# Scores moved directly behind a visit's transpositions, and first blocks' transposed tiles packed four to a PSUM bank, in a fused encoder and decoder layer

## The chip, the cores and the metric

The kernel runs on one NeuronCore of a Trainium2 chip. Its time is the device time of one execution in microseconds (us). Three executions of the kernel before gave 2728.57, 2730.44 and 2730.65, a median of 2730.44. Beside these stands one profiled execution, from which all rows of the profile come. Everything is computed in fp32.

## The reference

An encoder layer runs over a short context (2 x 77 x 512), and a decoder layer over 2 sequences of 2048 tokens, both with 16 heads of 32 and a feed-forward part of 2048. Cut to what matters:

```python
D, H, DFF, MD = (512, 16, 2048, 128)

def _rel_bias(emb, qlen, klen):
    rp = arange(klen)[None, :] - arange(qlen)[:, None]
    bucket = where(rp < 0, minimum(-rp, MD - 1), minimum(rp, MD - 1) + MD)
    return emb[bucket].transpose(2, 0, 1)

def _mha(xq, xkv, w_in, b_in, w_out, b_out, bias):
    q, k, v = ...                     # projections, 16 heads of 32
    scores = einsum('bhqd,bhkd->bhqk', q, k) / sqrt(32) + bias[None]
    attn = softmax(scores, axis=-1)
    out = einsum('bhqk,bhkd->bhqd', attn, v)
    return out.transpose(0, 2, 1, 3).reshape(Bq, Tq, D) @ w_out.T + b_out

x = src                               # the context, 2 x 77 x 512
x = x + _mha(_ln(x, ...), _ln(x, ...), ..., enc bias)
x = x + relu(_ln(x, ...) @ ff1.T + b1) @ ff2.T + b2
memory = x
y = tgt                               # 2 x 2048 x 512
yn = _ln(y, ...)
y = y + _mha(yn, yn, ..., _rel_bias(dec_rel_self, 2048, 2048) + causal)
y = y + _mha(_ln(y, ...), memory, ..., _rel_bias(dec_rel_cross, 2048, 77))
y = y + relu(_ln(y, ...) @ ff1.T + b1) @ ff2.T + b2
```

The change lies in the causal self-attention of the decoder. The relative bias is a constant for keys 127 or more positions back, so only the last two key tiles of a row of tiles need the bias added.

## The kernel before

**Units and pieces.** A sequence of 2048 tokens is cut into four blocks of 512 tokens, m = 0 to 3; the text calls them first to fourth block. The 16 heads make four groups g of four heads, and a block has four row tiles t of 128 tokens. One (sequence, m, g, t) is a unit, 128 of them (line 329). Unit (m, t) sees 4m + t + 1 key tiles of 128, and `pieces` (line 315) cuts these into pieces of at most four tiles. `stream` lists all pieces in order.

**The four operations on a piece.** `scores` (line 357) takes four banks of PSUM, one a head, and multiplies the queries of a head (32 rows of TensorE's array) with up to 512 keys into each (line 375). VectorE then reads each bank once, writes the scores to SBUF and reduces their maximum (line 384; line 391 for the last two tiles, with bias). After a unit's last piece one more reduction joins the maxima (line 401), and four exponentials on ScalarE, one a head, are put into a list, `late_exps`; `exps(k)` issues k of them (line 406). `turn` (line 412) transposes probabilities on TensorE, 128 x 128 at a time (line 426), into PSUM banks, and copies each bank to SBUF, on VectorE (line 431) or ScalarE (line 433). A bank normally holds one key tile of the four heads; in a first block it holds one head's key tiles, one to four. `values` (line 440) multiplies the transposed probabilities with the values (line 455) into a bank of its own, which is read out at the end of the visit.

**PSUM.** Eight banks make a ring (`bank`, line 180): each new bank is the one taken longest ago. TensorE waits where that bank has not been read yet.

**The order of the work.** It is written out by the main loop (from line 1883), one visit per pair of pieces of a unit. A unit of a first or second block has one visit; a unit of a third or fourth block has two (third block: seven or eight tiles, then 2, 2, 3 or 4; fourth: eight, then five to eight). Every engine runs its own instructions in this order. In a unit's last visit the order is: transpositions, then `slot(n + 1)`, then exponentials, then the scores of the unit two ahead (`score_next` for one piece, `score_two` for two), then the values. In an earlier visit there is no slot. `may_score` allows a piece only when the unit two before has turned the tiles whose place in SBUF it takes, since two units' probabilities alternate there.

**Slots.** `slot(n)` (line 1319) holds everything that is not attention between probabilities and values: first the light stages, then products, then late stages. Light and late stages are norms of later rows, the whole encoder (during the first sequence), the first part of the cross-attention, bias tiles, and sums and stores of weights for the feed-forward part; each has a planned slot. The products are the q, k, v and output projections of neighbouring blocks as one-level Strassen parts: `part_job` (products at line 1134) and `pair_job` (line 1048), with weights loaded two jobs ahead by `load_next` through SP's queue. `w2_store` and `w2_sums` (lines 1401 to 1432) prepare feed-forward weights on SP's queue and on POOL and reuse a buffer, so that the store of a half has to be issued ahead of the next sums.

After the last unit a stage of cross-attention and feed-forward follows, from about 1651 us of the span on, whose code is not touched.

Of the kernel before, what the change touches and what calls it, by code (L numbers as in the profile page):

```python
# [22 lines left out]
HC = P // HD  # L23
MB = 512
NMB = T // MB
TB = MB // P
# [28 lines left out]
def tile_encoder_decoder(ctx: ExitStack, tc: tile.TileContext, ins, out):  # L55
# [103 lines left out]
    with (  # L159
# [20 lines left out]
        def bank():  # L180

            ring.append(ring.pop(0))
            return psum[:, ring[-1], :]

        def in_turn(what, tile):
            i = count[what] % tile.shape[1]
            count[what] += 1
            return tile[:, i, :]
# [126 lines left out]
        def pieces(i):  # L315


            n = i + 1
            if n % 4 == 1 and n > 1:
                sizes = [4] * ((n - 5) // 4) + [3, 2]  # L320
            else:
                sizes = [4] * (n // 4) + ([n % 4] if n % 4 else [])
            out, k0 = [], 0
            for s in sizes:
                out.append((k0, s))
                k0 += s
            return out

        units = [(b, m, g, t) for b in range(B) for m in range(NMB) for g in range(NC) for t in range(TB)]
        stream = [(n, k0, kn) for n, u in enumerate(units) for k0, kn in pieces(u[1] * TB + u[3])]  # L330
# [78 lines left out]

        got = {}  # L410

        def turn(pieces):

            first = units[pieces[0][0]][1] == 0
            loads = []
            for n, k0, kn in pieces:
                ks = range(k0, k0 + kn)
                if first:
                    loads += [[(n, k, r) for k in ks] for r in range(HC)]
                else:  # L420
                    loads += [[(n, k, r) for r in range(HC)] for k in ks]
            for o, load in enumerate(loads):
                pt = bank()
                pts = in_turn("pts", pts_all).rearrange("p (x q) -> p x q", q=P)
                for x, (n, k, r) in enumerate(load):
                    nc.tensor.transpose(pt[:, ts(x, P)], state[n]["p"][r][:, k], ident)  # L426
                    got[n, k, r] = pts[:, x, :]
                w = len(load) * P
                free = pieces[0][0] == len(units) - 2 and (pieces[0][1] or o >= 4)
                if free or (o % 2 if first else o in (4, 6) if len(loads) == 8 else o >= (len(loads) + 1) // 2):  # L430
                    nc.vector.tensor_copy(pts[:, : len(load), :], pt[:, :w])  # L431
                else:
                    nc.scalar.copy(pts[:, : len(load), :], pt[:, :w])  # L433
                if not first and o == (7 if len(loads) == 8 else min(3, len(loads) - 1)):
                    exps(1)
            exps(HC if first else 0 if units[pieces[0][0]][1] == NMB - 1 else 1)

# [739 lines left out]
        NU = NC * TB  # L1177
        jobs = {n: [] for n in range(-1, len(units) + NU)}
        light = {n: [] for n in range(-1, len(units) + NU)}
        late = {n: [] for n in light}  # L1180

        for x, (b, m) in enumerate(blocks):
            u = x * NU
            first = m == 0
# [27 lines left out]
            for t in range(TB):  # L1212
                end = x == len(blocks) - 1
# [29 lines left out]
            for g in range(NC):  # L1243
# [4 lines left out]
                at = u + g * TB - 3  # L1248
# [67 lines left out]
            light[n].append(lambda kind=kind: wc_sums(sa_name[kind], True, spare, sa_from[kind]))  # L1316
            late[n + 1].append(lambda kind=kind: wc_store(sa_d[kind], spare))
        light[6].append(lambda: make_bias(2, rel, v))
        def slot(n):
            for f in light[n]:  # L1320
                f()
            for _, run, _ in jobs[n]:
                load_next()
                run(loaded[ran[0]])
                ran[0] += 1
            for f in late[n]:
                f()
            if n == 5:
                load_next()
# [62 lines left out]
        free = pp[:, 3 * HC * MB : END - 3 * HC * MB]  # L1392
# [28 lines left out]
        def w2_store(c, part):  # L1421

            def store(z0, z1, name, src):
                u = SUBS.index(name)
                nc.sync.dma_start(w2_d[z0:z1, u, :, ts(c, P)].rearrange("z p o -> p z o"), src)

            if part == 0:
                for n in ("11", "21", "22"):
                    store(0, 7, n, tens[:, :7, int(n[0]) - 1, ts(int(n[1]) - 1, P)])
            (z0, z1), t = list(ones.items())[part]  # L1430
            for k in range(4):
                store(z0, z1, f"T{k + 1}", t[:, k])
# [25 lines left out]
            late[u + 8].append(lambda dst=dst, z=z: wc_store(dst, z))  # L1458
        u = 2 * NU
        for c, k in enumerate((0, 2, 4, 10)):  # L1460
            light[u + k + 2].append(lambda c=c: w2_store(c, 1))
            late[u + k + 1].append(lambda c=c: w2_store(c, 0))
        for c, k in enumerate((0, 2, 4, 10)):
            light[u + k].append(lambda c=c: w2_sums(c))
        u = 6 * NU
# [381 lines left out]
        end = len(units)  # L1847
        size = [m * TB + t + 1 for b, m, g, t in units]
        turned_to, scored_to, at = {n: 0 for n in range(end)}, {}, [0]
# [11 lines left out]
        def score_next():  # L1861
            n, k0, kn = stream[at[0]]
            scores(n, k0, kn)
            scored_to[n] = k0 + kn
            at[0] += 1

        def score_two():

            n, k0, kn = stream[at[0]]
            at[0] += 1  # L1870
            both = may_score()
            at[0] -= 1
            if both and stream[at[0] + 1][0] == n and stream[at[0] + 1][2] < kn:
                scores(*stream[at[0] + 1])
                scores(n, k0, kn)
                scored_to[n] = size[n]
                at[0] += 2
            else:
                score_next()
                if both:  # L1880
                    score_next()
# [1 line left out]
        score_next()  # L1883
        score_next()
        slot(0)
        i = 0
        while i < len(stream):
            n = stream[i][0]
            pair = [p for p in stream[i : i + 2] if p[0] == n]
            while scored_to.get(n) != size[n]:  # L1890
                score_next()
            while any(u == n for u, _ in late_exps):
                exps(1)
            ends = pair[-1][1] + pair[-1][2] == size[n]
            turn(pair)
            if n == end - 2:
                for _, k0, _ in pair:
                    feed(k0 + 4)
            turned_to[n] = pair[-1][1] + pair[-1][2]
            third = units[n][1] == 2  # L1900
            if third and ends:
                exps(2)
            if ends and n + 1 < end:
                slot(n + 1)
            if not third:
                exps((0, 2, 1, 1)[units[n][1]])
            if may_score():
                if units[n][1] and (len(pair) > 1 or third):
                    score_two()
                else:  # L1910
                    score_next()
            if third and not ends:
                exps(1)
            values(pair)
            while may_score() and (len(pair) > 1 or units[n][1] == 0):
                score_next()
            if third and not ends:
                exps(1)
            i += len(pair)
# [68 lines left out]
```

## Time and profile before

| what | value |
|---|---|
| three executions | 2728.57, 2730.44, 2730.65 us |
| profiled execution | 2728.76 us, span 2726.9 us |
| granted TensorE clock, mean | 0.998 |
| instructions in the span | 68245 |
| TensorE matmuls / weight loads | 2707.0 us (99%) / 2214.9 us (81%), 26606 each |
| VectorE (DVE) | 1842.0 us (68%), 5402 |
| ScalarE (ACT) | 1534.6 us (56%), 2994 |
| GpSimd (POOL) | 1000.8 us (37%), 844 |
| HBM | 140 GB/s over the span |

All times inside the span are counted from its start. The first sequence's four blocks of self-attention begin at 28.4, 162.4, 370.1 and 590.0 us, the second's at 853.7, 991.2, 1185.2 and 1405.2; the last ends at 1651.1. The busy time of TensorE (PE) is modelled from when matmuls end, so a matmul that waits for a bank or for an operand can count as busy. PEld is the load of the stationary operand. In the views, a row of a group has the line, engine, operation, destination and source with their shapes, the count, the busy time and mean duration, and in brackets the idle time of the engine just before and what ended it. A table by stretches has the start and end, the length, then for PE and PEld the busy time with the number of instructions in brackets, the granted clock, the busy share of the DMA engines, and their GB/s. In a row of the chain or of an engine's timeline the first number is the start and the second the duration of the run of instructions.

### The profile page before, as it was taken

To read this page: it belongs to the slowest core of one execution; us is meant where nothing else is said; L and a number is where in the kernel's file an instruction comes from. 1 tells how busy PE (TensorE), PEld (TensorE's weight loads), DVE (VectorE), ACT (ScalarE), POOL (GpSimd) and SP (SyncE) were. 2 spreads that over 40 slices of the span, in tenths; PEclk is the share of its full clock that TensorE was granted. 3 is DMA by queue.
4 is the path that set the end of the run, shared out by engine and by line. 5 is a ranking of instruction groups with operands and counts; after the bars stand their busy time and mean duration, and the time that the engine had idled before them with its cause. 6 is when DMAs were issued, how large, how long until landed. Compare 5 with 4: busy or idle time off the path is not lost.

```text
span 2726.9 us, 68245 instructions
## 1 busy us (share of the span) xinstructions
PE 2707.0 (99%) x26606; PEld 2214.9 (81%) x26606; DVE 1842.0 (68%) x5402; ACT 1534.6 (56%) x2994; POOL 1000.8 (37%) x844
## 2 busy tenths in 40 slices
PE   9999999999999999999999999999999999999998
PEld 6678877777876677777777777898989898989898
DVE  5776688888875687788888793646464746464645
ACT  3544567777786547667777784444444444444431
POOL 2602235500300513322300203455556565656456
PEclk9999999999999999999999999999999999999999
DMA  8724345511213522342411206565657565656465
GB/s 241 210 94 137 126 148 170 170 51 43 67 45 88 138 81 67 111 137 91 132 50 35 79 16 222 171 214 172 213 171 239 168 216 169 218 167 218 151 223 185
DMA packets 296276, 385.10 MB, mean 141 GB/s; under 512 B 41184, under 2 KB 165648, under 8 KB 295826
## 3 DMA queue, kind: packets, MB, share of 16 engines
q1 hardware_dynamic: 295954, 380.73, 44.7%
q8 instruction: 211, 3.46, 0.5%
q14 instruction: 111, 0.91, 0.1%
HBM read 334.15 MB, written 46.47 MB: 140 GB/s over the span
## 4 chain that ended last, share of the span: by engine, by line
PE 95%; DVE 2%; ACT 1%; issue 1%; POOL 1%; DMA 1%; SPq 0%; POOLq 0%; DVEq 0%; ACTq 0%
PE psum L426 18%; PE psum L1632 14%; PE psum L1661 13%; PE psum L375 11%; PE psum L455 9%; PE psum L1134 8%; PE psum L1795 3%; PE psum L1752 3%; PE psum L1048 3%; PE psum L865 2%; PE psum L835 1%; PE psum L873 1%; PE psum L589 1%; PE psum L810 1%; PE psum L239 1%; PE psum L215 1%
## 5 line engine op out<-in xcount | busy, mean ns | idle before, releaser
L406 ACT ACTIVATE pp<-pp,nm 128x128 f32<-128x128 f32 (+15 forms) x512 | 611.8, 1201 | 31.9 <-DVE nm L401 31.3
L384 DVE TENSOR_SCALAR_CACHE_REDUCE pp<-psum 128x512 f32<-128x512 f32 (+3 forms) x1024 | 556.2, 590 | 53.5 <-PE psum L375 51.3
L433 ACT COPY pts<-psum 128x512 f32<-128x512 f32 (+2 forms) x730 | 382.4, 580 | 311.6 <-PE psum L426 270.5
L426 PE MATMUL psum<-ident,pp 128*128 128x128 f32 x4352 | 530.5, 276 | 5.9 <-ACT nT L310 3.2
L426 PEld LDWEIGHTS psum<-ident,pp 128*128 128x128 f32 x4352 | 472.1, 141 | 58.9 <-DVE pp L384 21.6
L375 PE MATMUL psum<-kT,q 32*128 32x512 f32 (+3 forms) x2560 | 332.9, 559 | 2.1 <-ACT nT L310 0.7
L455 PEld LDWEIGHTS psum<-pts,vv 128*32 128x32 f32 x8704 | 226.2, 110 | 127.3 <-DVE pp L384 55.4
L431 DVE COPY pts<-psum 128x512 f32<-128x512 f32 (+3 forms) x406 | 252.1, 654 | 81.7 <-PE psum L426 79.2
L1661 PE MATMUL psum<-pp 128*128 128x128 f32 x2560 | 304.5, 276 | 1.9 <-POOL pp L961 1.6
L1661 PEld LDWEIGHTS psum<-pp 128*128 128x128 f32 x2560 | 296.3, 192 | 8.6 <-issue 2.8
L455 PE MATMUL psum<-pts,vv 128*32 128x128 f32 x8704 | 279.3, 275 | 0.7 <-DVE mx L391 0.3
L961 POOL TENSOR_TENSOR pp<-pp 128x512 f32<-128x512 f32 x159 | 212.7, 1354 | 112.2 <-DMA pp<-in_dec_ff_wT_dram 51.5
L1632 PE MATMUL psum<-vv,pp 128*128 128x256 f32 x1024 | 236.2, 381 | 0.0
L375 PEld LDWEIGHTS psum<-kT,q 32*128 32x128 f32 x2560 | 145.0, 183 | 104.7 <-issue 38.5
L1632 PEld LDWEIGHTS psum<-vv,pp 128*128 128x128 f32 x1024 | 190.3, 190 | 25.8 <-issue 0.5
L391 DVE CUSTOM_DVE_ANT_0 pp<-psum,bias 128x256 f32<-128x256 f32 (+1 forms) x512 | 195.9, 411 | 19.8 <-PE psum L375 19.8
L1645 DVE TENSOR_TENSOR kT<-kT,psum 128x512 f32<-128x512 f32 x96 | 65.8, 686 | 191.1 <-PE psum L1632 190.9
L1648 ACT ACTIVATE kT<-kT,vecs 128x256 f32<-128x256 f32 x192 | 87.0, 501 | 156.7 <-DVE kT L1645 156.0
L1632 PE MATMUL psum<-nT,pp 128*128 128x256 f32 x768 | 174.1, 380 | 0.0
L1632 PEld LDWEIGHTS psum<-nT,pp 128*128 128x128 f32 x768 | 144.2, 190 | 20.3 <-issue 1.6
L1669 ACT COPY oT<-psum 128x128 f32<-128x128 f32 x56 | 15.0, 267 | 239.0 <-PE psum L1661 239.0
L493 POOL TENSOR_TENSOR oT<-rirows,oT 128x512 f32<-128x512 f32 x30 | 38.4, 1279 | 288.2 <-DMA rirows<-rec 154.6
(274 smaller groups left out, 4106.8 us busy)
## 6 DMA issues: line engine op xcount, KB each, us to landing
pp<-w_d SPq DMA_DIRECT2D x520, 256.0 KB
pp<-in_dec_ff_wT_dram SPq DMA_DIRECT2D x112, 256.0 KB
bias<-tzg SPq DMA_DIRECT2D x128, 128.0 KB
pp<-wo_d SPq DMA_DIRECT2D x56, 256.0 KB
wqk<-in_dec_sa_in_wT_dram SPq DMA_DIRECT2D x52, 256.0 KB
wqk<-sa_q SPq DMA_DIRECT2D x84, 128.0 KB
vv<-in_enc_ff_wT_dram SPq DMA_DIRECT2D x8, 1024.0 KB
xr<-in_x_dram SPq DMA_DIRECT2D x32, 256.0 KB
```

The source lines that it names most:

```text
L375: nc.tensor.matmul(banks[r][:, : kn * P], q[rows4(r), ts(t, P)], kT[rows4(r), g, k0 * P : (k0 + kn) * P], start=True, stop=True,)
L384: nc.vector.tensor_scalar(p[:, k0 : k0 + far], s[:, :far], 1.0, None, ALU.mult, ALU.max, accum_out=st["mx"][:, r, c : c + 1],)
L391: nc.vector.tensor_tensor_reduce(p[:, k0 + far : i + 1], s[:, far:kn], near[:, 2 - (kn - far) :], 1.0, LOWEST, ALU.add, ALU.max, accum_out ...
L406: nc.scalar.activation(p, p, AF.Exp, bias=nm, accum_out=to)
L426: nc.tensor.transpose(pt[:, ts(x, P)], state[n]["p"][r][:, k], ident)
L431: nc.vector.tensor_copy(pts[:, : len(load), :], pt[:, :w])
L433: nc.scalar.copy(pts[:, : len(load), :], pt[:, :w])
L455: nc.tensor.matmul(ot[rows4(r)], vv[:, k, ts(g * HC + r, HD)], got.pop((n, k, r)), start=k == k0 and (whole or not begun), stop=k == k1 - ...
L961: engine.tensor_tensor(out, a, b, ALU.subtract)
L1134: nc.tensor.matmul(mm[:, ts(f, TOK)], left[:, c, ts(f, P)], right[:, c, :], start=c == 0, stop=c == 1,)
L1632: nc.tensor.matmul(mm[:, ts(f, TOK)], a[:, c, ts(f, P)], b[:, c, :], start=fresh and f == 0 and c == 0, stop=c == 1, skip_group_check=True,)
L1661: nc.tensor.matmul(psum[:, bank_i, ts(col, P)], lhs[:, c, :], w[:, c, :], start=fresh and k in (0, 3) and c == 0, stop=c == 3, skip_group_ ...
```

## The change

There are two parts.

The first is in `turn`. In first blocks the heads' key tiles are put in one row, head by head, and cut into banks of four: a unit with 1, 2, 3 or 4 key tiles takes 1, 2, 3 or 4 banks, where it took four each time. The division of the copies between the two engines also changes. In a first block the odd banks still go to VectorE. In other blocks, with `left` the number of banks that still follow, VectorE copies every other bank (`left % 2`) if the visit before ended with a slot that had products (`fresh`); otherwise banks 4 and 6 of eight, as before, and of fewer than eight banks the last but one, where it was the second half of them. One exponential that was issued behind the fourth bank (or the last, if there are fewer, or the eighth of eight) is issued behind the last.

The second is in the main loop. In a unit's last visit in the second, third and fourth blocks (`scored`) the slot runs after the scores: transpositions, exponentials, scores, slot, values. Inside such a slot the products come first, then the light stages, then the late ones. Four stores of weights (`w2_store(c, 1)`) move from the light stages to a new list, `ahead`, which stays in front of the products. When `score_two` has two pieces and the visit is such a one, it takes the longer piece first, where it took the shorter first if both belong to one unit. First blocks keep the old order, as do visits that don't end a unit.

```diff
@@ -409,14 +409,15 @@
 
         got = {}
 
-        def turn(pieces):
+        def turn(pieces, fresh):
 
             first = units[pieces[0][0]][1] == 0
             loads = []
             for n, k0, kn in pieces:
                 ks = range(k0, k0 + kn)
                 if first:
-                    loads += [[(n, k, r) for k in ks] for r in range(HC)]
+                    heads = [(n, k, r) for r in range(HC) for k in ks]
+                    loads += [heads[o : o + TB] for o in range(0, len(heads), TB)]
                 else:
                     loads += [[(n, k, r) for r in range(HC)] for k in ks]
             for o, load in enumerate(loads):
@@ -427,11 +428,12 @@
                     got[n, k, r] = pts[:, x, :]
                 w = len(load) * P
                 free = pieces[0][0] == len(units) - 2 and (pieces[0][1] or o >= 4)
-                if free or (o % 2 if first else o in (4, 6) if len(loads) == 8 else o >= (len(loads) + 1) // 2):
+                left = len(loads) - 1 - o
+                if free or (o % 2 if first else left % 2 if fresh else o in (4, 6) if len(loads) == 8 else left == 1):
                     nc.vector.tensor_copy(pts[:, : len(load), :], pt[:, :w])
                 else:
                     nc.scalar.copy(pts[:, : len(load), :], pt[:, :w])
-                if not first and o == (7 if len(loads) == 8 else min(3, len(loads) - 1)):
+                if not first and not left:
                     exps(1)
             exps(HC if first else 0 if units[pieces[0][0]][1] == NMB - 1 else 1)
 
@@ -1177,7 +1179,7 @@
         NU = NC * TB
         jobs = {n: [] for n in range(-1, len(units) + NU)}
         light = {n: [] for n in range(-1, len(units) + NU)}
-        late = {n: [] for n in light}
+        late, ahead = {n: [] for n in light}, {n: [] for n in light}
 
         for x, (b, m) in enumerate(blocks):
             u = x * NU
@@ -1316,13 +1318,16 @@
             light[n].append(lambda kind=kind: wc_sums(sa_name[kind], True, spare, sa_from[kind]))
             late[n + 1].append(lambda kind=kind: wc_store(sa_d[kind], spare))
         light[6].append(lambda: make_bias(2, rel, v))
-        def slot(n):
-            for f in light[n]:
+        def slot(n, scored=False):
+            for f in ahead[n] + ([] if scored else light[n]):
                 f()
             for _, run, _ in jobs[n]:
                 load_next()
                 run(loaded[ran[0]])
                 ran[0] += 1
+            if scored:
+                for f in light[n]:
+                    f()
             for f in late[n]:
                 f()
             if n == 5:
@@ -1458,7 +1463,7 @@
             late[u + 8].append(lambda dst=dst, z=z: wc_store(dst, z))
         u = 2 * NU
         for c, k in enumerate((0, 2, 4, 10)):
-            light[u + k + 2].append(lambda c=c: w2_store(c, 1))
+            ahead[u + k + 2].append(lambda c=c: w2_store(c, 1))
             late[u + k + 1].append(lambda c=c: w2_store(c, 0))
         for c, k in enumerate((0, 2, 4, 10)):
             light[u + k].append(lambda c=c: w2_sums(c))
@@ -1864,13 +1869,13 @@
             scored_to[n] = k0 + kn
             at[0] += 1
 
-        def score_two():
+        def score_two(long_first):
 
             n, k0, kn = stream[at[0]]
             at[0] += 1
             both = may_score()
             at[0] -= 1
-            if both and stream[at[0] + 1][0] == n and stream[at[0] + 1][2] < kn:
+            if both and not long_first and stream[at[0] + 1][0] == n and stream[at[0] + 1][2] < kn:
                 scores(*stream[at[0] + 1])
                 scores(n, k0, kn)
                 scored_to[n] = size[n]
@@ -1883,7 +1888,7 @@
         score_next()
         score_next()
         slot(0)
-        i = 0
+        i, fresh = 0, False
         while i < len(stream):
             n = stream[i][0]
             pair = [p for p in stream[i : i + 2] if p[0] == n]
@@ -1892,7 +1897,7 @@
             while any(u == n for u, _ in late_exps):
                 exps(1)
             ends = pair[-1][1] + pair[-1][2] == size[n]
-            turn(pair)
+            turn(pair, fresh)
             if n == end - 2:
                 for _, k0, _ in pair:
                     feed(k0 + 4)
@@ -1900,15 +1905,19 @@
             third = units[n][1] == 2
             if third and ends:
                 exps(2)
-            if ends and n + 1 < end:
+            scored = ends and n + 1 < end and units[n][1] > 0
+            if ends and n + 1 < end and not scored:
                 slot(n + 1)
             if not third:
                 exps((0, 2, 1, 1)[units[n][1]])
             if may_score():
                 if units[n][1] and (len(pair) > 1 or third):
-                    score_two()
+                    score_two(scored)
                 else:
                     score_next()
+            fresh = scored and len(jobs[n + 1]) > 0
+            if scored:
+                slot(n + 1, True)
             if third and not ends:
                 exps(1)
             values(pair)
```

## The prediction

> **What bounds the kernel now.** I read the page first (busy shares, chain), then scores alone by block, the chain row by row, and the engines' timelines.
>
> ```profile
> PE 2707.0 (99%) x26606; PEld 2214.9 (81%) x26606; DVE 1842.0 (68%) x5402; ACT 1534.6 (56%) x2994; POOL 1000.8 (37%) x844
> ...
> PE 95%; DVE 2%; ACT 1%; issue 1%; POOL 1%; DMA 1%; SPq 0%; POOLq 0%; DVEq 0%; ACTq 0%
> ```
>
> TensorE carries the chain; nothing else can set the end for long. But its busy time is modelled and hides waits, so I look at how long the same work takes in different visits. Rows are start, duration, engine and line; L426 is a transposition, L1134/L1048 a slot's product, L375 scores, L455 values.
>
> ```profile
> 1192.61 5.18 PE psum L1134 x24
> 1197.80 1.91 PE psum L375 x16
> 1199.70 0.57 PE psum L455 x16
> 1200.28 4.30 PE psum L426 x32
> 1204.58 1.93 PE psum L375 x16
> 1206.51 1.89 PE psum L455 x64
> 1208.39 1.02 PE psum L426 x8
> 1209.41 3.46 PE psum L1134 x16
> 1212.87 1.07 PE psum L375 x8
> 1213.94 0.57 PE psum L455 x16
> 1214.51 3.66 PE psum L426 x32
> ```
>
> These give a law for undisturbed work. Scores: 8 take 1.07 and 16 take 1.93, so 0.86 for a piece of 512 keys (0.215 a tile of 128) and 0.21 once a run. Transpositions: 8 take 1.02, 32 take 3.66, so 0.11 each and 0.14 once. Values: (1.89 - 0.57)/48 = 0.0275 each and 0.13 once. Products: (5.18 - 3.46)/8 = 0.215 each and 0.02 once. What exceeds this is a wait: 4.30 for 32 transpositions holds 0.64 of it.
>
> What such waits are shows in a second-block visit whose scores, pieces of 512 and 384 keys (0.21 + 0.86 + 0.645 by the law), run 2.6 over:
>
> ```profile
> 1050.40 4.30 PE psum L375 x16
> ```
>
> ```profile
> 1048.31 0.69 DVE L883 TENSOR_TENSOR pp<-psum,pp 128x512 f32<-128x512 f32 x1 [3.02 <-PE psum L882]
> ...
> 1050.33 4.37 PE L375 MATMUL psum<-kT,q 32*128 32x384 f32 x16
> ...
> 1051.45 0.29 PEld L375 LDWEIGHTS psum<-kT,q 32*128 32x128 f32 x2 [0.61 <-DVE pp L845]
> ```
>
> VectorE idled 3.02 us during the slot's products; then products, other stages and scores came at once, and the scores waited for banks that VectorE had not read. All PSUM banks go round one ring of eight: each new bank is the one taken eight before it.
>
> Next, scores by block (start:end, length, then PE busy), second, third and fourth block of either sequence:
>
> ```profile
> 162.40:370.10 207.70, 33.83 (x273) 15.39 (x272) 1.00 0.40 124
> 370.10:590.00 219.90, 50.33 (x401) 21.39 (x400) 1.00 0.48 144
> 590.00:853.70 263.70, 60.81 (x464) 27.34 (x464) 1.00 0.16 48
> ...
> 991.20:1185.20 194.00, 41.82 (x276) 17.94 (x272) 0.99 0.30 91
> 1185.20:1405.20 220.00, 50.37 (x401) 21.41 (x400) 1.00 0.33 105
> 1405.20:1651.10 245.90, 59.21 (x448) 26.73 (x448) 1.00 0.20 64
> ```
>
> By the program's order a second block has 18 runs and 112 tiles of scores: 18 x 0.21 + 112 x 0.215 = 27.9. Two take 33.83 + 41.82, which is 19.9 more. A third has 32 and 176 (44.6), so 11.6 more for two; the fourths have 58 and 413 together (101.0), 19.0 more. Busy time runs past the chain's piece by 0.07 a run (4.37 against 4.30 above), so 17, 7 and 15 are waits. The other pieces, by the same law, hold some 9, 5 and 3. Together **26, 12 and 18 us**: the most that the new order can win, about 2%.
>
> **The change part by part.**
>
> *Order, second block (32 visits).* One head's maxima of a piece, on VectorE:
>
> ```profile
> 1316.27 0.69 DVE L384 TENSOR_SCALAR_CACHE_REDUCE pp<-psum 128x512 f32<-128x512 f32 x1
> ```
>
> Scores now come right after transpositions, when VectorE is idle, and their maxima (0.69 a piece and head by this row) run under the products. In the visit above the maxima would run from about 1045 to 1050, the other stages' reductions follow to 1056; values come at 1053 and only the next visit's VectorE copies come late, some 0.8 of today's 3.3. I leave a quarter, 7 of 26: **-19**. Bounds: 0 and 13 left.
>
> *Order, fourth block (32 ending visits, 23 with products).* Where no products stand between, the trace already has the new order:
>
> ```profile
> 807.80 0.29 PEld L375 LDWEIGHTS psum<-kT,q 32*128 32x128 f32 x2 [0.26 <-DVE pts L431]
> ```
>
> ```profile
> 806.46 1.28 DVE L431 COPY pts<-psum 128x512 f32<-128x512 f32 x2
> ```
>
> The last head waits for the second of two VectorE copies. The new split leaves one copy there (`left == 1`), ending at about 807.1, before the scores ask. I leave 2 of 18: **-16**; bounds 0 and 8.
>
> *Order, third block (32 ending visits).* Here it can lose. A unit's first visit turns 7 or 8 tiles, its ending visit only 2, 3 or 4: too few to hide anything, and today the products stand in the gap. A visit with almost no products (one norm's transpositions, about 0.5) shows what remains:
>
> ```profile
> 1316.10 0.60 PEld L375 LDWEIGHTS psum<-kT,q 32*128 32x128 f32 x6 [0.17 <-issue]
> 1317.02 0.29 PEld L375 LDWEIGHTS psum<-kT,q 32*128 32x128 f32 x2 [0.32 <-DVE pp L384]
> ```
>
> The row of 1316.27 above is the eighth and last maximum of the visit before, done at 1316.96, and with it the fourth head's bank comes free. Directly behind the transpositions (1315.57) the scores would take banks one earlier in the ring and need the seventh, done with its reading-out as the eighth begins (1316.35): 0.75 in each visit with t=1. ScalarE matters where two pieces, or products, follow and reach the banks of the visit's own tiles:
>
> ```profile
> 537.68 1.02 PE psum L426 x8
> ...
> 581.79 1.90 PE psum L426 x16
> ```
>
> ```profile
> 583.35 0.69 DVE L384 TENSOR_SCALAR_CACHE_REDUCE pp<-psum 128x512 f32<-128x512 f32 x1
> ```
>
> ```profile
> 539.84 0.58 ACT L433 COPY pts<-psum 128x512 f32<-128x512 f32 x1
> ```
>
> ```profile
> 583.65 1.69 ACT L406 ACTIVATE pp<-pp,nm 128x1664 f32<-128x1664 f32 x1
> ...
> 585.33 1.06 ACT L433 COPY pts<-psum 128x512 f32<-128x512 f32 x2
> ```
>
> t=0: transpositions end at 538.70, the second piece wants its banks at 539.66, ScalarE's copy (behind four exponentials) ends at 540.42: 0.75. The new split of the seven tiles before can put ScalarE 0.8 later, so 0.75 to 1.55; I take the row as it stands. t=3: ends at 583.69, eighth maximum at 584.04: 0.4; after 0.64 of scores the first product takes the bank of the first tile, whose copy ends at 585.9: 1.2 more. t=2, by the same rows with a piece of 384: about 0.45. Sum 3.55 for six of eight groups of heads. In the last group two pieces of the next block follow at t=2 and t=3 and wait for more of ScalarE's copies: 2.1 and 2.3, so 5.9. In all 6 x 3.55 + 2 x 5.9 = 33, in place of 12: **+21**. Bounds 8 (only t=1 and the 0.4) and 48 (ScalarE late everywhere).
>
> *One more entry.* Transpositions and products use the whole array, scores and values quarters of it; going from transpositions to products costs 0.02. With scores between, products pay an entry of their own: 0.10 (between 0.02 and 0.14 of the law). Of 95 moved slots 88 have TensorE work: **+9**, bounds 2 and 12. The Trainium skill ("TensorEngine Tiling (Array Packing)", Key Properties) says that a change of tiling mode drains the array; by its "TensorE: Matmul & The Clock Gate" (Single matmul latency) a warm drain and issue is 166 ns, an estimate of 15 us in place of 9, and a sum of -2. The intercepts agree with the rule, not with that size.
>
> *First blocks.* For 1, 2 and 3 key tiles the four heads' transpositions fill 1, 2 and 3 banks instead of 4: 6 copies fewer a group of heads, 48 in all. TensorE's work stays 0.11 each.
>
> These copies, 0.58 for a full bank on ScalarE by the row of 539.84, lie beside products of 3.5 us and more; only the few waits for a busy engine go. I take **-3**, bounds -8 and +2 (a bank of four heads is copied only when all are turned).
>
> *At nothing.* The other copies' new split and the exponentials moved behind the last load: queued engine time, priced above where it is waited for. SP and POOL pass no scores: POOL's order among itself is kept; on SP a slot's weight loads now precede its light loads, and `ahead` keeps four weight stores in front. Light stages start some 2 to 5 us later; their takers are a slot (over 10 us) on, and a bias tile is fetched three slots early.
>
> **Sum.** -19 - 16 + 21 + 9 - 3 = -8. The profiled run took 2728.76 (span 2726.9 and 1.9 around it), which gives 2720.8; the median 2730.44 stands 1.7 higher, so **2722**.
>
> **The rivals.**
>
> *Slower by the third block.* One mechanism: its short visits wait for banks behind four exponentials and eight maxima. At the bound of 48 instead of 33 the sum is -19 - 16 + 36 + 9 - 3 = +7: 2738. It turns the sign from 41 on and is beyond 0.2% (5.5 us, about what a measurement of this kernel can tell from no change) from 46.5. For it: ScalarE's rows, and third-block scores that today wait hardly at all. Against: VectorE and ScalarE catch up under the products that now follow. The Trainium skill has it as a rule: tiling speeds TensorE, not the emptying of PSUM ("TensorEngine Tiling (Array Packing)", PSUM Bottleneck); the 0.32 above agrees.
>
> *The third block absorbs it.* New waits of 12, the present amount: -29, 2701. For it: a larger VectorE share of copies after a slot (`fresh`). Against: rows 1316.10 to 1317.02.
>
> *Nothing.* The waits only change place; gains of 25 meet 21 + 9 - 3: 2730, within 0.2%.
>
> **How the numbers follow.** Forecast 0.36 (own range 2712 to 2725), absorbed 0.14, nothing 0.18, slower 0.32. Faster 0.50, same 0.18, slower 0.32. The range 2702 to 2745 reaches nearly to the absorbed case and past the slower one, where also half of the second block's waits stay (13 for 7, 2744).
>
> **What would show it.** Second and fourth block: L375 busy falls to 29 to 32 and to 52 to 54, and the two stretches shorten by some 9 and 7 us each. Third block: L375 rises from 50 towards 60 and the stretch grows by some 10, with L375 or a product's weight load waiting for `pts` L433 or `pp` L384. Third-block scores still at 50 would make me too high; second-block rows of 4 us that persist, or values waiting for copies, too low.

## The result and the profile after

The changed kernel takes 2761.91 us (median; 2753.12 to 2771.32), the kernel before beside it 2730.52 (2728.57 to 2730.65): a ratio of 1.012, 95% interval 1.0103 to 1.0137, or 31 us slower. The forecast was 2722, and the range ended at 2745.

The page of the changed kernel, its profiled execution being the longest of its runs (2771.32 us):

```profile
span 2769.5 us, 68159 instructions
PE 2725.9 (98%) x26606; PEld 2232.6 (81%) x26606; DVE 1878.9 (68%) x5424; ACT 1522.4 (55%) x2924; POOL 1002.0 (36%) x844
...
PE 92%; ACT 3%; DVE 2%; DMA 1%; issue 1%; POOL 1%; SPq 0%; DVEq 0%; ACTq 0%; POOLq 0%
```

TensorE still carries the chain, but ScalarE has gone from 1% to 3% of it. Scores by block, the same view as in the prediction (start:end, length, PE busy, PEld busy, granted clock, DMA share, GB/s), second, third and fourth block of either sequence:

```profile
162.80:371.50 208.70, 29.90 (x276) 14.85 (x272) 1.00 0.36 118
371.50:614.20 242.70, 60.35 (x404) 25.91 (x400) 0.97 0.45 135
614.20:878.10 263.90, 55.17 (x464) 26.38 (x464) 1.00 0.15 47
...
1016.60:1203.90 187.30, 32.22 (x273) 16.25 (x272) 1.00 0.29 88
1203.90:1446.60 242.70, 60.17 (x404) 25.83 (x400) 0.97 0.30 99
1446.60:1693.20 246.60, 54.01 (x448) 25.69 (x448) 1.00 0.20 64
```

The scores did what was forecast: down in second blocks (33.83 and 41.82 to 29.90 and 32.22) and in fourth blocks (60.81 and 59.21 to 55.17 and 54.01), up in third blocks (50.3 to 60.3). The stretches did not follow:

| stretch | before, us | after, us | difference |
|---|---|---|---|
| first blocks | 134.0 and 137.5 | 134.4 and 138.5 | +1.4 |
| second blocks | 207.7 and 194.0 | 208.7 and 187.3 | -5.7 |
| third blocks | 219.9 and 220.0 | 242.7 and 242.7 | +45.5 |
| fourth blocks | 263.7 and 245.9 | 263.9 and 246.6 | +0.9 |
| after the attention | 1075.8 | 1076.3 | +0.5 |

All of the loss is in the third blocks, and their granted clock is 0.97, where it was 1.00. Here is one of their ending visits (the one that completes a unit and has the slot) with t=0 in the chain (start, length, what), and behind it a visit with t=1:

```profile
1271.04 0.58 PE psum L427 x4
1271.62 1.35 ACT pp L406 x2
1272.96 0.15 ACT oT L470
1273.12 1.36 ACT pp L406 x2
1274.47 0.48 ACT pts L435
1274.95 0.04 issue
1274.99 0.91 PE psum L375 x2
1275.90 1.24 PE psum L1050 x4
...
1278.15 4.59 PE psum L427 x32
...
1286.56 1.02 PE psum L427 x8
1287.58 1.79 PE psum L375 x8
1289.37 3.65 PE psum L1136 x16
1293.02 0.57 PE psum L457 x16
1293.60 3.64 PE psum L427 x32
```

At t=0 the chain leaves TensorE for ScalarE's exponentials and its copy of a turned tile. The timeline of the same moment (the idle time before a row and its releaser in brackets):

```profile
1268.82 1.36 ACT L406 ACTIVATE pp<-pp,nm 128x1280 f32<-128x1280 f32 x1
...
1270.18 1.35 ACT L406 ACTIVATE pp<-pp,nm 128x1280 f32<-128x1280 f32 x1
...
1271.52 1.35 ACT L406 ACTIVATE pp<-pp,nm 128x1280 f32<-128x1280 f32 x1
...
1273.01 1.37 ACT L406 ACTIVATE pp<-pp,nm 128x1280 f32<-128x1280 f32 x1
...
1274.37 0.57 ACT L435 COPY pts<-psum 128x512 f32<-128x512 f32 x1
...
1274.99 0.29 PEld L375 LDWEIGHTS psum<-kT,q 32*128 32x128 f32 x2 [1.53 <-ACT pts L435]
```

The last head's scores wait for the bank of the visit's second turned tile, and ScalarE copies it only behind four exponentials of 1.35 us. By the prediction's law the 16 score matmuls take 1.71 us; from 1271.99 to the products' start at 1275.83 are 3.84, so the wait is 2.1. Soon after, the granted clock falls to half for 3.4 us, while TensorE works without a gap (the last three values of a line are clock, DMA share and GB/s):

```profile
1270.00:1275.00 5.00, 4.09 (x63) 2.61 (x52) 4.37 (x16) 4.94 (x10) 4.92 (x5) 1.00 0.58 169
...
1276.00:1277.00 1.00, 1.00 (x4) 0.51 (x4) 1.00 (x9) 0.00 (x0) 1.00 (x2) 0.83 1.02 377
1277.00:1278.00 1.00, 1.00 (x17) 0.60 (x16) 0.96 (x8) 0.00 (x0) 0.49 (x1) 0.50 0.38 141
...
1279.00:1280.00 1.00, 1.00 (x6) 1.00 (x6) 0.69 (x1) 0.00 (x0) 0.00 (x0) 0.50 0.01 4
1280.00:1281.00 1.00, 1.00 (x11) 1.00 (x10) 0.40 (x1) 0.59 (x1) 0.00 (x0) 0.96 0.00 0
```

The 32 transpositions at 1278.15 take 4.59 us, where the row of 1293.60 has as many in 3.64. The third blocks of this execution have eight such drops, six behind waits at t=0 and two behind t=3 of the last group; those of the kernel before have none.

### The profile page after: what moved, and what is told of

Its sections match the earlier page's. It is cut to its first block, busy times and chain, and to the rows that moved or that the text cites. A ratio compares the mean times of both kernels' runs of the same rounds, so it can differ in the third digit from the quotient of the medians.

```text
span 2769.5 us, 68159 instructions
## 1 busy us (share of the span) xinstructions
PE 2725.9 (98%) x26606; PEld 2232.6 (81%) x26606; DVE 1878.9 (68%) x5424; ACT 1522.4 (55%) x2924; POOL 1002.0 (36%) x844
## 3 DMA queue, kind: packets, MB, share of 16 engines
q8 instruction: 211, 3.46, 0.5%
## 4 chain that ended last, share of the span: by engine, by line
PE 92%; ACT 3%; DVE 2%; DMA 1%; issue 1%; POOL 1%; SPq 0%; DVEq 0%; ACTq 0%; POOLq 0%
PE psum L427 17%; PE psum L1637 14%; PE psum L1666 12%; PE psum L375 9%; PE psum L1136 9%; PE psum L457 9%; PE psum L1800 3%; PE psum L1757 3%; PE psum L1050 3%; ACT pp L406 2%; PE psum L867 2%; PE psum L837 1%; PE psum L875 1%; PE psum L591 1%; PE psum L812 1%; DVE pp L384 1%
## 5 line engine op out<-in xcount | busy, mean ns | idle before, releaser
L435 ACT COPY pts<-psum 128x512 f32<-128x512 f32 x660 | 370.3, 592 | 368.6 <-PE psum L427 355.0
L433 DVE COPY pts<-psum 128x512 f32<-128x512 f32 x428 | 290.1, 689 | 109.1 <-PE psum L427 105.9
L375 PE MATMUL psum<-kT,q 32*128 32x512 f32 (+3 forms) x2560 | 329.9, 558 | 12.0 <-ACT pts L435 10.2
L375 PEld LDWEIGHTS psum<-kT,q 32*128 32x128 f32 x2560 | 150.2, 183 | 107.3 <-issue 32.9
```

Source lines behind the costliest of these rows:

```text
L375: nc.tensor.matmul(banks[r][:, : kn * P], q[rows4(r), ts(t, P)], kT[rows4(r), g, k0 * P : (k0 + kn) * P], start=True, stop=True,)
```

## The experiments

Theory A: the loss is made in third blocks, by long waits for ScalarE's copies and by the lower clock that follows them. Theory B: it is spread, by the entries and waits of every moved slot. Where a time "before" is given beside a result, it is the kernel before on the same chip.

**Third blocks in the old order.**

```diff
-            scored = ends and n + 1 < end and units[n][1] > 0
+            scored = ends and n + 1 < end and units[n][1] in (1, 3)
```

> The change, but third blocks keep the old order (slot between transpositions and scores). Theory A: the loss lies in the third blocks alone (their two stretches grew from 219.9 to 242.7 us each in the profile of the changed kernel, all other stretches together shrank by about 3). Then the time is 2725 to 2729 and the clock is back at 0.998. Theory B: the extra entry of the products (about 0.2 us a moved slot by the visits' rows) and waits cost everywhere; then 2735 or more stays.

Measured: 2725.48 us (2723.17 to 2726.63), before 2729.01; ratio 0.9983 (0.9974 to 0.9993). Its scores in the two third blocks, with their stretches:

```profile
370.40:591.50 221.10, 51.97 (x404) 21.21 (x400) 1.00 0.51 149
...
1180.60:1401.40 220.80, 51.59 (x404) 21.04 (x400) 1.00 0.36 110
```

The stretches are back at 221 us and a clock of 1.00. Theory A holds for the place: the third blocks' new order costs some 35 us, and what is left of the change wins 3.5, where the prediction's other steps made some 30.

**Third blocks, t=0: both turned tiles copied by VectorE.**

```diff
-                if free or (o % 2 if first ...
+                b, m, g, t = units[pieces[0][0]]
+                both = m == 2 and t == 0 and len(loads) == 2
+                if free or both or (o % 2 if first ...
```

> The change, but in the ending visit of a third block's first row tile (t=0, 8 visits) both turned tiles are copied by VectorE, none by ScalarE. Theory A: the 2.1 us that the second piece's scores wait there are ScalarE's copy behind four exponentials (its copy ends at 1274.94, VectorE's would at about 1273.2), and the lower clock follows from that wait. Then some 1.7 us of each of the 8 waits go (-14) and the clock loss of these visits with it: 2740 to 2750. Rival: VectorE's maxima hold these banks anyway, the copy only lengthens VectorE's queue: within 5 us of the changed kernel's 2762.

Measured: 2749.75 us (2748.75 to 2752.06). The timeline of the same visit as above:

```profile
1254.83 1.28 DVE L435 COPY pts<-psum 128x512 f32<-128x512 f32 x2
1254.98 0.31 PEld L375 LDWEIGHTS psum<-kT,q 32*128 32x128 f32 x8 [0.17 <-issue]
1254.98 2.10 PE L375 MATMUL psum<-kT,q 32*128 32x512 f32 x16
```

The scores run 2.10 us (in the changed kernel they began at 1271.99 and ended at 1275.90), which leaves a wait of 0.3, so the maxima were hardly in the way: the rival falls. Eight copies moved from one engine to the other give back 10 to 12 us, with the clock's part in it.

**Third blocks with the old division of copies and the old place of the exponential.**

```diff
-                if free or (... left % 2 if fresh else o in (4, 6) if len(loads) == 8 else left == 1):
+                if free or (... left % 2 if fresh and not third else o in (4, 6) if len(loads) == 8
+                    else o >= (len(loads) + 1) // 2 if third else left == 1):
...
-                if not first and not left:
+                if not first and (o == (7 if len(loads) == 8 else min(3, len(loads) - 1)) if third else not left):
```

> The change, but visits of third blocks divide the copies and place the exponential as the kernel before does (seven tiles: the last three on VectorE, one exponential behind the fourth copy). Theory A: ScalarE's four exponentials start some 1.2 us earlier, the wait at t=0 falls from 2.1 towards 0.8: -8 to -11, and fewer clock drops: 2742 to 2755. Rival: only the place of the slot matters: 2758 to 2766.

Measured: 2747.03 us (2746.0 to 2752.26).

```profile
1253.34 2.76 PE L375 MATMUL psum<-kT,q 32*128 32x512 f32 x16
...
1254.54 0.59 ACT L436 COPY pts<-psum 128x512 f32<-128x512 f32 x1
...
1255.18 0.30 PEld L375 LDWEIGHTS psum<-kT,q 32*128 32x128 f32 x4 [0.68 <-ACT pts L436]
```

The wait at t=0 is 1.0, in place of 2.1 (2.76 less the 0.07 by which busy time runs past the chain's piece, against 1.71 by the prediction's law). So ScalarE stood near where the prediction read it in the trace of before (0.75); the new division and the later exponential together put it more than a microsecond further back. No run separates the two.

**First blocks' banks alone**, on the kernel before.

```diff
-                    loads += [[(n, k, r) for k in ks] for r in range(HC)]
+                    heads = [(n, k, r) for r in range(HC) for k in ks]
+                    loads += [heads[o : o + TB] for o in range(0, len(heads), TB)]
```

> The kernel before with only the first blocks' tiles packed four to a bank (48 copies fewer); order, division of copies in other blocks and exponentials as before. The prediction took -3 for it (bounds -8 and +2). In the changed kernel the two first-block stretches were 0.4 and 1.0 us longer than before, so the rival is no gain: 2729 to 2732.

Measured: 2725.82 us (2724.64 to 2730.66) against 2729.01; ratio 0.9992 (0.9982 to 1.0001). The median moves by the predicted 3, but the interval touches no change, so this run alone does not settle it. Profiles can't settle it either: the first sequence's first block took 132 to 138 us in profiled executions that all had the new banks.

**Third blocks: only the 18 visits with one piece of scores behind them**, and **only the 8 with t=0**, in the new order.

```diff
+            scored = ends and n + 1 < end and (units[n][1] in (1, 3) or units[n][1] == 2 and units[n][2] < 3 and units[n][3] > 0)
...
+            scored = ends and n + 1 < end and (units[n][1] in (1, 3) or units[n][1] == 2 and units[n][3] == 0)
```

> The change, but of the third blocks' 32 ending visits only the 18 keep the new order in which one piece of scores follows (t=1 to 3 of the first three groups of heads). By the changed kernel's rows these wait 0.72, 0.23 and 0.47 us and pay 0.2 us more for entries; the long waits (2.1 to 2.5 us) are gone. Theory A (long waits, and the lower clock behind them, carry most of the loss): some 10 us above the 2725.5 with third blocks in the old order, 2733 to 2738, clock 0.998 or more. Rival (any moved slot of a third block costs about the same): 18/32 of 36 us, 2745 or more.

> The change, but of the third blocks' ending visits only the 8 with t=0 keep the new order. Theory A: their waits of 2.1 us (in place of about 0.5 to 0.8) and 0.2 us of entry make +14, clock loss up to +8 more: 2737 to 2747, at a clock of 0.996 to 0.998. Rival (all alike): 8/32 of 36 us, 2734 to 2735.

Measured: 2733.32 us (2732.27 to 2736.41) for the first and 2737.55 (2732.03 to 2739.02) for the second, 8 and 12 above the version with third blocks in the old order. That is 0.4 a visit with one piece and 1.5 a visit with t=0; "all alike" would be 1.1 for each and falls. The second kernel lies at the lower end of what was expected, and shows the clock by itself: in its profiled execution, with the eight waits of 2.0 to 2.1 us in it, it took 2732.0 at a mean clock of 1.000; another took 2735.2 at 0.999, and the other four 2737.3 to 2739.0 at 0.997 to 0.998.

**The last group's t=2 and t=3 in the old order** (4 visits), and **the changed kernel once more** beside it.

```diff
+            scored = ends and n + 1 < end and units[n][1] > 0 and not (units[n][1] == 2 and units[n][2] == 3 and units[n][3] > 1)
```

> The change, but the last group of heads of a third block keeps the old order at t=2 and t=3 (4 visits). There two pieces of the next block follow and wait 2.2 and 2.5 us. Theory A: with entries and clock these 4 visits carry 11 to 15 us of the loss, so it runs that much below the changed kernel beside it, 2744 to 2751. Rival (spread evenly over the 32 visits): 4 to 5 us below it.

> The changed kernel once more, beside the others on the same chip. Its four runs so far went from 2753.1 at a clock of 0.998 to 2771.3 at 0.993. If the lower clock is a loss of its own and not a sign of longer waits, time again falls with the clock within these runs, by some 3 to 4 us a thousandth; without it all runs lie within 3 us.

Measured: 2749.73 us (2745.91 to 2758.2) and, for the changed kernel, 2760.02 (2757.35 to 2764.58). Four visits carry 10 us by the medians, a little under the 11 to 15 expected and twice what an even spread would give. The two sets of runs scatter so much that they overlap, but the profiles bear the medians out: clear of the drops of the clock (1.7 us each, see below) the third blocks' stretches are some 4 us shorter in either sequence, 8 for the four visits without the drops behind them. What stands there in the changed kernel, at t=3:

```profile
1438.06 1.55 ACT L435 COPY pts<-psum 128x512 f32<-128x512 f32 x3
1438.68 0.29 PEld L375 LDWEIGHTS psum<-kT,q 32*128 32x128 f32 x2 [1.53 <-ACT pts L435]
```

Over both sets of runs of the changed kernel time falls as the clock rises: 2771.3 at 0.993, 2764.6 at 0.995, 2758.5 to 2763.6 at 0.996 to 0.997, 2757.4 and 2753.1 at 0.998. The waits themselves do not vary: at t=0 the scores' run, from its first matmul to the next run's first, takes 3.84 or 3.69 in all eight visits of both profiles, but six of the first profile's and three of the second's are followed by half the clock. The third blocks' stretches go by the number of these drops: 242.7 us with four of them, 241.0 with three, 239.5 with two, some 1.7 us for each. So the clock is a loss of its own.

**Without the new division where a visit follows a slot without products**, third blocks in the old order.

```diff
-                if free or (... else left == 1):
+                if free or (... else o >= (len(loads) + 1) // 2):
```

> The change with third blocks in the old order, and the copies of visits that follow a slot without products divided as the kernel before does (the second half of fewer than eight banks on VectorE). If the new division (one bank on VectorE, more on ScalarE) makes the transpositions of a fourth block's last group wait (0.8 us in three visits, against 0.1 before), the time falls by 2 to 4 us to 2721 to 2724; if these waits come from the order of the other stages, it stays within 1 us of 2725.5.

Measured: 2722.65 us (2719.01 to 2725.39), before 2728.31; ratio 0.9976 (0.9967 to 0.9986). 2.8 below the version with the new division, which is the time that was expected, but by luck: the reason was another. The waits of the transpositions in fourth blocks do go (three of 0.8 us in the last group of the first sequence become 0.0 to 0.1), but scores then wait for copies instead: L375 takes 58.95 and 57.74 us there, against 55.15 and 53.84 in the version with the new division, and the two fourth blocks are as long as with it (264.1 against 264.0 us, 249.1 against 248.9, each up to the last run of values). What got shorter are the third blocks, from 221.1 and 220.8 to 219.6 and 219.7: in the old order their visits follow no moved slot, and there the new division had made scores wait 1.4 to 1.5 us in two of the four visits with t=0 of each block, where the kernel before has 0.3 and 1.0.

**One part of the new order alone: products stay in front of the scores**, only light and late stages move behind them.

```diff
+            moved = ends and n + 1 < end and units[n][1] > 0
             if ends and n + 1 < end:
-                slot(n + 1)
+                slot(n + 1, "products" if moved else "all")
...
+            if moved:
+                slot(n + 1, "rest")
             values(pair)
```

> The kernel before with one part of the new order alone: in blocks two to four the products stay directly behind the transpositions, and only the light and late stages move behind the scores. If the second blocks' waits come from other stages' VectorE work ahead of the maxima, these go here too, without the second entry of the products: some 7 to 12 us less in the second sequence's second block, the third blocks unchanged, 2716 to 2723. Rival (the scores must come directly behind the transpositions, so that maxima run under products): the waits stay, 2727 to 2731, or the values then wait for copies.

Measured: 2742.83 us (2740.02 to 2747.02); ratio 1.0058 (1.0043 to 1.0073). Neither expectation had this time. The two first blocks are 5.6 and 6.4 us longer and the first sequence's second block 3.6. The timeline of TensorE shows, in a first block and in a second one:

```profile
885.83 6.21 PE L215 MATMUL psum<-nT,wqk 128*128 128x512 f32 x8 [4.28 <-DMA wqk<-in_dec_sa_in_wT_dram]
...
1135.25 1.13 PE L1048 MATMUL psum<-xt,wqk 128*128 128x256 f32 x4 [2.06 <-POOL xt L961]
```

Products that stay early now wait for what the other stages deliver later: sums of POOL, and weights whose loads SP's queue issues late (from 882.99 on for the first row; that the moved loads hold them up is a reading of the queue's order, not shown by a run). For the question that was asked, the waits of the scores, the first expectation was right: in the second sequence's second block L375 takes 35.92 us, against 41.82 before and 32.22 in the changed kernel. So about six tenths of what the new order takes from the scores there come from setting the other stages behind them, with the products still in front. In the first sequence's second block there is no such gain (35.82, against 33.83 before and 29.90). In the change itself the products move back with these stages, and no such wait is in the third blocks, where the loss is.

**The new order in second blocks only**, with first blocks' banks, the old division and the old place of the exponential elsewhere: in the second sequence alone, and in both.

```diff
+            scored = ends and units[n][:2] == (1, 1)
...
+            scored = ends and units[n][1] == 1
```

> First blocks' tiles packed four to a bank, and the new order only in the second sequence's second block (16 visits); elsewhere the old order, division of copies and place of the exponentials. That stretch was 6.9 us shorter with the new order, the banks took 3 off the median: 2717 to 2721, faster than the kernel before and than all versions so far. If the banks' share does not hold, 2721 to 2724.

> As the version with the second sequence's second block alone, and the first sequence's as well. In the profiles that stretch was 0.9 us longer with the new order: 0 to 2 us above the other version. If the order pays in every second block, as the prediction had it (-19 over both), it is 2 or more below.

Measured: 2719.06 us (2716.99 to 2719.96), ratio 0.9963 (0.9948 to 0.9978), and 2719.85 (2717.44 to 2721.06), ratio 0.9967 (0.9955 to 0.998); before 2729.22. The first is 10 us faster than the kernel before, and no kernel here has a lower median. All its runs lie in the range that was set for banks that hold their 3 us, and below the one for banks that do not, which speaks for the banks. The first sequence's second block adds nothing to it.

## Why the prediction was wrong

The reading of the profile was right: which waits exist, that the new order takes some of them from the scores of second and fourth blocks, that third blocks can lose, and there for ScalarE's copies. The rival "slower by the third block" has the place and the sign of what happened, but its price, 2738, was far too low: the third block's waits stayed within its bound of 48, and the other terms did not hold.

Laying the prediction's law against every run of TensorE's instructions in the changed kernel gives its terms, the clock kept apart (they also follow from the stretches: second blocks -5.7, less 32 entries of 0.19, are -12; third blocks 45.5, less as many entries and eight drops of the clock of 1.7, are 26):

| step | predicted, us | measured, us |
|---|---|---|
| second block, order | -19 | -12 |
| fourth block, order | -16 | -3 |
| third block, order | +21 | +26 |
| one more entry | +9 | +17 |
| first blocks | -3 | -3 (median; interval from -5 to 0) |
| lower clock | not there | 0 to 18 over the runs; 6 to 7 at the median, as what the rest leaves of 31 |

Without the clock that is +25; 2753.1 us at a clock of 0.998 stands 24.4 above the profiled 2728.8 of before. The clock is what lies above that, in the runs with a lower one. Of the 40 us between the forecast and the result the order of the fourth blocks has 13, the entries 8, the order of the second blocks 7, the clock 6 to 7 and the order of the third blocks 5. So no one term failed alone; the largest miss is the gain of fourth blocks, and the only term that was left out altogether is the clock.

*One more entry* is a step that was sized wrong. The prediction took 0.10 and no more than 0.14. The same 16 products in two visits with t=1 of a third block, in the chain before and after:

```profile
1260.75 3.46 PE psum L1134 x16
1264.20 1.07 PE psum L375 x8
1265.27 0.58 PE psum L455 x16
```

They take 3.46 when they follow the transpositions and 3.65 (row 1289.37 above) between scores and values: 0.19, on top of the 0.02 they paid already. Both changes of the array's tiling, into the products and out of them, cost a tenth; only one had been counted. From start to start of the runs in the two profiles, undisturbed products exceed the law by about 0.0 between two runs on the whole array, by 0.07 to 0.10 with scores on one side, and by 0.18 to 0.20 between scores and values. With 88 slots that is 17. The Trainium skill's figure for a warm drain and issue ("TensorE: Matmul & The Clock Gate", Single matmul latency, 166 ns), which the prediction set aside as too large, gives an estimate of 15 and was the better of the two.

*Order, second and fourth block.* The scores' own waits fell, from 18 to 11 and from 15 to 8 us, but less far than foreseen: after a slot with products the last tiles' copies end on ScalarE, and scores directly behind the transpositions wait for them, 0.2 to 0.5 in most visits. In fourth blocks, above all in their last groups, the transpositions wait some 4 us more, since the new division leaves ScalarE one copy more where no products cover it. That is an exchange, as the version without it shows: there these waits go, and the scores' waits are back at 14. So under either division the new order wins next to nothing in fourth blocks. "I leave 2 of 18" went by the one copy that the old rows show last. In the one second block that gained time, the second sequence's, the products' part of the mechanism, maxima that run under them, was the smaller one: the version with products in front keeps six tenths of the gain on the scores.

*Order, third block.* The sum of waits, 33, was nearly that of the rows, 36, but partly by luck. At t=1 it was 0.72 a visit (predicted 0.75), in the last group 2.2 and 2.5 (2.1 and 2.3), at t=3 otherwise 0.47 in place of 1.6. At t=0 it was 2.1: "I take the row as it stands", 0.75, and an upper end of 1.55 were both too low. The old row nearly holds with the old division of the seven tiles before and the old place of the exponential, as the third experiment shows with 1.0.

*The clock* is the step that was missing altogether, and by itself it would have carried the time past 0.2%. The trace of before has it, behind the 0.99 in the prediction's own row of the second sequence's second block: a visit there whose scores wait 2.2 us (from 1109.2 on) is followed by half the clock.

```profile
1105.00:1112.00 7.00, 7.00 (x77) 4.79 (x74) 5.81 (x17) 6.36 (x14) 0.84 (x1) 1.00 0.73 227
...
1114.00:1117.00 3.00, 3.00 (x39) 2.61 (x32) 1.78 (x11) 0.75 (x4) 2.92 (x3) 0.50 0.23 87
```

With that row every new wait of two microseconds could have had a second price; of the two longest waits of scores in the kernel before this one has it, and the 2.6 us at 1050.40 have not.

"At nothing" held for SP and POOL: the stretch behind the attention is as long as before, and TensorE has no wait for either in the third blocks. It did not hold for the copies' new split, which the prediction named beside them: that is the wait at t=0 and the transpositions' waits above.

Of the marks set out in advance, L375 in second blocks (29.90 and 32.22, predicted 29 to 32) and in third blocks (60, predicted "towards 60") came true and in fourth blocks nearly (55.17 and 54.01 against 52 to 54); of the stretches that were to shorten by 9 and 7 only the second sequence's second block did, by 6.7, and that of the third grew by 23 in place of 10.

## What to carry to other kernels

Work that covers a wait in one stage can be moved only where the engines that empty the banks have finished: read for each kind of visit when the last copy ends, and under the new division of the copies, not the old one. Count both changes of tiling that a moved block of matmuls pays, before it and after it, from two rows of the trace with the same matmuls. And move the part that the rows favour: here one block of eight holds nearly all that the new order won.

## What the runs showed that was not expected

A wait of about two microseconds on TensorE can halve its clock for the next 3 to 4 us of work, and whether it does varies from one execution to the next. In the two profiles of the changed kernel 8 and 5 such drops lie in the third blocks, all of them behind waits of 1.97 us or more, of which there are 12; in the experiments' profiles no third-block wait of 1.5 or less has one behind it. That is no threshold: in the second sequence's first block a drop follows scores that wait 1.6 us, in the kernel before too (at 980.6). In the kernel with t=0 alone the profiled execution had none, behind the same eight waits. A drop costs up to 1.7 us, as the chain shows behind the wait of 1438.68 above, with 16 products that take 3.65 elsewhere:

```profile
1440.35 5.34 PE psum L1136 x16
```

By the profile TensorE was idle for only 0.9 us in the visit shown first (first row of the clock's table). But busy time is modelled and can hold a wait, so how much of the 2.1 us the array stood still is not shown.

The Trainium skill ("TensorE: Matmul & The Clock Gate", HAM oscillation) warns of idle gaps above about 3.4 us; this trace differs, with drops behind waits of 2.0 to 2.7 us. The same page ("What's actually happening") has the activity measured in a window that runs freely, which would fit a drop that comes in one execution and not in the next; no run here shows the window.

Second, a block of full-array matmuls between quarter-array ones costs 0.1 us at each of its two ends (0.19 for both), of which the prediction's sum had only one.
